# A fused Hawk and RWKV layer on one core: the channel mix's key by seven products, x added by an accumulating DMA, engine order by a table

## The chip, the core and the metric

The kernel runs on one core of a Trainium2 chip. The core has a matrix engine (TensorE, PE in the profile, with PEld for its weight loads), a vector engine (VectorE, DVE), a scalar engine (ScalarE, ACT), a general engine (GpSimd, POOL) and a queue engine (SyncE, SP). Each engine works through its own list of instructions in order; semaphores tie the lists together. PE writes into eight accumulation banks of 128 x 512 fp32 (PSUM); everything else lies in on-chip memory (SBUF). The metric is the device time of one launch in microseconds (us), lower is better: the median of three runs before the change is 652.33 (652.04 to 652.97).

## What is computed

Eight samples of 1024 tokens with 256 channels. Each sample is normalized, and two branches of the normalized input are added to x. The reference, cut to what matters:

```python
def hawk(xn):                                  # 384 hidden channels
    gate = xn @ Wg.T;  u = xn @ Wi.T
    y = causal_depthwise_conv(u, conv_w) + conv_b          # 4 taps
    ig = sigmoid(y @ lru_Wi.T + lru_bi)
    rg = sigmoid(y @ lru_Wg.T + lru_bg)
    alpha = exp(-8 * softplus(lam) * rg)
    beta = sqrt(1 - alpha**2 + 1e-6)
    h = scan(h = alpha * h + beta * ig * y)    # along the tokens
    return (gelu(gate) * h) @ Wo.T

def channel_mix(xn):                           # 256 channels
    xr = mu_r * xn + (1 - mu_r) * previous_token(xn)
    xk = mu_k * xn + (1 - mu_k) * previous_token(xn)
    r = sigmoid(xr @ W_r.T)
    k = relu(xk @ W_k.T) ** 2
    return r * (k @ W_v.T)

xn = layernorm(x)
out = x + hawk(xn) + channel_mix(xn)           # fp32 throughout
```

## The kernel before

**Layout and rounds.** Hidden channels lie on the 128 partitions and tokens along the free axis, in two halves of 512 (`HALVES`). The kernel goes through one round per sample: a first round (sample 0), six middle ones and a last one. Round s computes u, gate, key, r and v products of sample s and the first two of three `l` groups, transposes and normalizes sample s+1, and finishes the recurrence and output products of sample s-1 (`chain`, `outs`). The last round does the whole recurrence of its own sample too.

**Seven products.** The input projections (family "u": Wi and Wg) and the two gate projections (family "l") are taken in pairs of 128 output rows. A pair of rows by two token halves and two channel blocks is a 2x2 block product, computed with seven block products in place of eight (the class `Group`). It needs sums of weight blocks (`weight_sums`) and sums of token blocks (`token_sums`: four subtractions of 128x512 on GpSimd). A group runs in steps on PE: step 1 starts the banks A and C; `seed` (ScalarE) copies A into a new bank B, and `five` copies C into SBUF; step 2 finishes A and adds to B; `fork_c` (VectorE) writes B + five into C; step 3 adds to B and C; `fork_d` writes B + five into the fourth output; step 4 finishes B. `evict` moves a finished bank out on ScalarE and gives it back. "l" has a third channel block, which is added plainly, and so a bank D and a step 5. The key of the channel mix is computed plainly: `key` takes a bank and two products for each of two row blocks and two halves, `key_relu` evicts it, `key_square` squares a half.

**Output.** `r_tanh` writes tanh of r into `tf`, which is the memory of the token sums `xsum`. `value` (VectorE) multiplies it by the v product. `load_again` loads x a second time into `res`, `add_value` adds 0.5 x `tf` to it, and `add_hawk` adds the output product and issues the store.

**Order.** There is no scheduler. `at(t, f)` notes a step at a time t, in units of one 128x512 product; `pe` notes a step of PE at a running clock; at the end all steps are sorted by t and called, and each appends its instructions to the lists of its engines. So the times in `at` only set the order within an engine. In the kernel before, they are offsets written out by hand beside each step: for example the lines `at(4.05, x_sums)`, `mixing(4.2, 5.5, "k")`, and in `Group.step` an eviction 0.1 after the product that ends it. Banks are handed out first in, first out (`take`, `give`), in the order in which steps are called.

**Start.** Before the first round, sample 0 is loaded, its first half normalized and transposed; the second half follows inside the first round (`prepare(1)`, `turn(1)` at 3.99, which copies the transposed half into `xnT`, one channel block on ScalarE and one on VectorE).

Of the kernel before, what the change touches and what calls it, by code (L numbers as in the profile page):

```python
# [12 lines left out]
P = 128  # L13
# [6 lines left out]
HC = 3  # L20
# [9 lines left out]


@with_exitstack
def kernel(
# [47 lines left out]
    ress = [fixed(f"res{n}", [TT, D]) for n in range(2)]  # L81
# [9 lines left out]


    xsum = fixed("xsum", [4, NT])
    ysum = fixed("ysum", [4, NT])
    tf = xsum.rearrange("p a b -> p (a b)").rearrange("p (t d) -> p t d", d=D)
# [54 lines left out]
    ROWS = {"i": ("u", 0), "g": ("u", HC), "lg": ("l", 0), "li": ("l", HC)}  # L150
    families = {"u": fixed("w_u", [DC, 2 * HC * P]), "l": fixed("w_l", [HC, 2 * HC * P])}
    sums = {n: fixed(f"sum_{n}", [4, HC, P]) for n in families}
# [5 lines left out]
    def rows_of(pair, apart):  # L158
        return (pair, pair + HC) if apart else (2 * pair, 2 * pair + 1)

# [11 lines left out]
    def token_sums(dst, b11, b12, b21, b22, pair=None):  # L172

        nc.gpsimd.tensor_tensor(dst[:, 0, :], b12, b11, ALU.subtract)  # L174
        nc.gpsimd.tensor_tensor(dst[:, 2, :], b22, dst[:, 0, :], ALU.subtract)
        nc.gpsimd.tensor_tensor(dst[:, 1, :], b22, b12, ALU.subtract)
        nc.gpsimd.tensor_tensor(dst[:, 3, :], b21, dst[:, 2, :], ALU.subtract)
# [8 lines left out]
    end_of = {}  # L186

    def at(t, f, *args):
        steps.append((t, len(steps), f, args))

    def pe(name, length, f, *args):
        at(clock[0], f, *args)
        clock[0] += length
        end_of[name] = clock[0]
# [4 lines left out]
    class Group:  # L199
# [7 lines left out]

        def step(self, n):
# [9 lines left out]
            def s1():  # L218
                bank["A"], bank["C"] = take(), take()
                product(bank["A"], A(0, 0), chunk(0, 0), start=True)  # L220
                product(bank["C"], S[0], T[:, 0, :], start=True)
# [10 lines left out]
            def s2():  # L232
                product(bank["A"], A(0, 1), chunk(1, 0))
                if third:
                    product(bank["A"], A(0, 2), third(0))
                product(bank["B"], S[1], T[:, 2, :])

            def fork_c():
                nc.vector.tensor_tensor(banks[bank["C"]], banks[bank["B"]], self.five, ALU.add)  # L239

            def s3():
                product(bank["B"], S[2], T[:, 1, :])
                product(bank["C"], S[3], chunk(1, 1))
                if third:
                    product(bank["C"], A(0, 2), third(1))
# [9 lines left out]
            def s4():  # L255
                product(bank["B"], A(1, 1), T[:, 3, :])
                if third:
                    product(bank["B"], A(1, 2), third(0))

            def s5():  # L260
                product(bank["D"], A(1, 2), third(1))
# [6 lines left out]
            if n == 1:  # L268
                pe(f"{self.name}.1", 2, s1)
                at(t + 1.1, seed)  # L270
                at(t + 2.1, five)
            elif n == 2:
                pe(f"{self.name}.2", 2 + extra, s2)
                at(t + 1.1 + extra, evict, "A", 0, 0)
                at(now() + 0.1, fork_c)
                self.after_c = now() + 0.1
            elif n == 3:
                assert t > self.after_c
                pe(f"{self.name}.3", 2 + extra, s3)
                at(t + 1.1, fork_d)  # L280
                self.after_d = t + 1.1
                at(now() + 0.1, evict, "C", 0, 1)
                if not third:
                    at(t + 2.0, self.out, 1, 1, "sbuf")
            elif n == 4:
                assert t > self.after_d
                pe(f"{self.name}.4", 1 + extra, s4)
                at(now() + 0.1, evict, "B", 1, 0)
            else:
                assert t > self.after_d  # L290
                pe(f"{self.name}.5", 1, s5)
                at(now() + 0.1, evict, "D", 1, 1)

    def plain(name, family, pair, chunk, chunks, out):


        def one(r, h):
            b = held[r, h] = take()
            for c in range(chunks):
                product(b, block(family, 2 * pair + r, c), chunk(c, h), start=(c == 0))  # L300

        def evict(r, h):
            b = held.pop((r, h))
            out(r, h, banks[b])
            give(b)

        held = {}
        for h in range(2):
            for r in range(2):
                pe(f"{name}.{r}{h}", chunks, one, r, h)  # L310
                at(now() + 0.1, evict, r, h)
# [27 lines left out]
    def u_group(s, gi):  # L339
        place = u_out(s)  # L340
        return Group(
            f"u{gi}_{s}",
# [4 lines left out]
            xsum,  # L347
# [3 lines left out]
    def l_group(s, gi):  # L351
        rows = rows_of(gi, s == B - 1)
        return Group(
            f"l{gi}_{s}",
# [4 lines left out]
            ysum,  # L359
            lambda r, h, src: l_out(rows[r], h, src),  # L360
            third=lambda h: y[:, 2, HALVES[h]],
        )

# [6 lines left out]

    def load_again(s):
        nc.sync.dma_start(ress[s % 2], x[s].rearrange("(t p) d -> p t d", p=P))
# [52 lines left out]
    def x_sums():  # L425
        def half(c, h):
            return xnT[:, c, 1 + h * NT : 1 + (h + 1) * NT]

        token_sums(xsum, half(0, 0), half(0, 1), half(1, 0), half(1, 1))

    def y_sums():
        def half(c, h):
            return y[:, c, HALVES[h]]

        token_sums(ysum, half(0, 0), half(0, 1), half(1, 0), half(1, 1))
# [16 lines left out]
    def key(m, h):  # L452
        b = take()
        for c in range(DC):
            product(b, weights["k"][:, c, m * P : (m + 1) * P], mixes["k"][:, c, HALVES[h]], start=(c == 0))
        kbank[m, h] = b

    kbank = {}

    def key_relu(s, m, h):  # L460
        ka = key_home(s)
        b = kbank.pop((m, h))
        nc.scalar.activation(ka[:, m, HALVES[h]], banks[b], AF.Relu)
        give(b)

# [4 lines left out]
    def by_token(w, lhs, t, chunks, abreast=False):  # L470

        b = take()
        order = [(j, c) for j in range(2) for c in range(chunks)]
        if abreast:
            order.sort(key=lambda jc: jc[1])
        for j, c in order:
            nc.tensor.matmul(  # L477
                banks[b][:, j * D : (j + 1) * D],
                lhs[:, c, (t + j) * P : (t + j + 1) * P],
                weights[w][:, c, :],  # L480
                start=(j == 0 and c == 0),
                stop=True,
                skip_group_check=True,
            )
        return b
# [6 lines left out]
    def r_product(t):  # L492
        token_bank["r", t] = by_token("r", mixes["r"], t, DC)

    def r_tanh(t):
        b = token_bank.pop(("r", t))
        nc.scalar.activation(tf[:, t : t + 2, :], two_tiles(b), AF.Tanh, scale=0.5)
        give(b)

    def v_product(s, t):  # L500
        token_bank["v", t] = by_token("v", key_home(s), t, DC)

    def value(t):
        b = token_bank.pop(("v", t))
        o = tf[:, t : t + 2, :]
# [3 lines left out]
    def add_value(s, h):  # L509
        o = ress[s % 2][:, 4 * h : 4 * h + 4, :]  # L510
        nc.vector.scalar_tensor_tensor(o, tf[:, 4 * h : 4 * h + 4, :], 0.5, o, ALU.mult, ALU.add)

    def o_product(s, t):
        token_bank["o", s, t] = by_token("o", gs[s % 2], t, HC, s == B - 1 and t == 0)

    def add_hawk(s, t, pieces=1):
        b = token_bank.pop(("o", s, t))
        n = 2 // pieces
        for j in range(0, 2, n):
            o = ress[s % 2][:, t + j : t + j + n, :]  # L520
# [58 lines left out]
    def tp(s):  # L579
        for h in range(2):  # L580
            for c in range(DC):
                pe(f"t{c}{h}_{s}", 0.5, transposes, s, c, h)
                at(now() + 0.1, put_transposed, s, c, h)

    def keys(s, h, m):
        pe(f"k{m}{h}_{s}", 2, key, m, h)
        at(now() + 0.1, key_relu, s, m, h)
        if m == 1:
            at(now() + 0.7, key_square, s, h)

    def gates(s, t):
        pe(f"r{t}_{s}", 2, r_product, t)
        at(now() + 0.1, r_tanh, t)

    def values(s, t, add=0.6):
        pe(f"v{t}_{s}", 2, v_product, s, t)
        at(now() + 0.1, value, t)
        if t % 4 == 2:
            at(now() + add, add_value, s, t // 4)

    def outs(s, t, pieces=1, add=0):
        pe(f"o{t}_{s}", 3, o_product, s, t)
# [32 lines left out]
    with tc.manual_schedule():  # L635
# [50 lines left out]
        busy(4)  # L686
        at(0.02, parameters)
# [3 lines left out]
        at(4.05, x_sums)  # L691
        mixing(4.2, 5.5, "k")
        mixing(12.2, 18.2, "r")
        clock[0] = 0.0
        rate = None
        lgs = {}
        for s in range(B):
            b = now()
            first, last = s == 0, s == B - 1
            us = [u_group(s, n) for n in range(3)]  # L700
            ls = [l_group(s, n) for n in range(3)]
            before = lgs.get(s - 1)
            if first:
# [4 lines left out]
                keys(s, 0, 0)  # L708
                us[2].step(2)
                us[1].step(3)  # L710
                keys(s, 0, 1)
                us[2].step(3)
                us[1].step(4)
                keys(s, 1, 0)
                us[2].step(4)
                keys(s, 1, 1)
                gates(s, 0)
                gates(s, 2)
            else:
# [6 lines left out]
                keys(s, 0, 0)  # L726
                us[0].step(3)
                us[1].step(2)
                keys(s, 0, 1)
# [3 lines left out]
                keys(s, 1, 0)  # L733
                us[2].step(2)
                us[1].step(4)
                keys(s, 1, 1)
                us[2].step(3)
                gates(s, 0)
                gates(s, 2)
                us[2].step(4)  # L740
            at(b + 30, load_again, s)
# [9 lines left out]
            if not last:  # L751
# [6 lines left out]
                at(now() - 0.1, y_sums)  # L758
# [9 lines left out]
                if s + 2 < B:  # L768
# [4 lines left out]
                    at(now() + 11.3, stats, s + 2, 0, 4)  # L773
# [147 lines left out]
```

## Time and profile before

| | |
|---|---|
| time, median of three runs | 652.33 us (652.04 to 652.97) |
| profiled execution, its own time | 652.18 us |
| its span, first to last instruction | 650.4 us |
| granted TensorE clock | 1.000 |
| a middle round (266.31 to 345.52): length | 79.21 us |
| busy in it: PE, DVE, ACT, POOL | 79.21, 57.51, 53.58, 12.58 us |
| bytes read from and written to HBM | 19.94 MB, 8.39 MB |
| loads of x for the sum (`res`), from SP | 8 of 1024 KB, 5.5 us each to landing |

The span is the time between the first and the last instruction of the profiled execution; 1.8 us of the execution lie around it. A row of a timeline reads: start, length, engine, line of the kernel, operation, written tile <- read tiles, shapes, count of merged instructions, and in brackets the idle time before it with what ended it. A row of the chain of waits reads: start, length, engine, tile, line, count. A 128x512 product in fp32 appears as two MATMUL records. Ends of matmuls are modelled, so starts are the safer numbers on PE.

### The profile page before, as it was taken

How to read it: one execution, taken by the hardware profiler on the slowest of the kernel's cores; microseconds unless marked ns; L12 is line 12 of the kernel's file. 1: busy time of each engine (PE TensorE's matmuls, PEld its weight loads, DVE VectorE, ACT ScalarE, POOL GpSimd, SP SyncE). 2: the span in 40 equal slices, each digit the busy share in tenths (PEclk: the TensorE clock that was granted, in tenths of full speed). 3: DMA queues.
4: the chain of work that ended last, by engine and by line, in shares of the span. 5: the costliest groups of instructions: out<-in, count | busy, mean ns of one | idle time of the engine just before them, and what ended most of it. 6: DMA issues, size and time to landing. Idle time of an engine off the chain costs nothing.

```text
span 650.4 us, 5894 instructions
## 1 busy us (share of the span) xinstructions
PE 644.3 (99%) x2048; PEld 375.5 (58%) x2048; DVE 471.2 (72%) x602; ACT 431.9 (66%) x616; POOL 117.5 (18%) x86
## 2 busy tenths in 40 slices
PE   8999999999999999999999999999999999999997
PEld 4466445864468544675447754487544865457466
DVE  4787869846797557966589565994759945699487
ACT  3786878358773687826888178872788537883680
POOL 3705200430004300043000330022300323104000
PEclk9999999999999999999999999999999999999999
DMA  9401200032000310014000140001200012000003
GB/s 316 137 2 37 93 0 1 30 100 65 0 1 33 107 55 1 1 44 142 9 0 1 48 147 0 0 1 48 82 1 1 1 48 82 0 0 1 1 18 113
DMA packets 27550, 28.71 MB, mean 44 GB/s; under 512 B 1152, under 2 KB 27008, under 8 KB 27520
## 3 DMA queue, kind: packets, MB, share of 16 engines
q1 hardware_dynamic: 27104, 27.92, 13.2%
q10 hardware_dynamic: 416, 0.41, 0.2%
q8 instruction: 16, 0.26, 0.2%
q14 instruction: 14, 0.11, 0.1%
HBM read 19.94 MB, written 8.39 MB: 44 GB/s over the span
## 4 chain that ended last, share of the span: by engine, by line
PE 97%; DVE 2%; ACT 0%; issue 0%; DVEq 0%
PE bank L180 64%; PE bank L477 30%; PE bank L403 2%; PE bank L660 1%; DVE y L540 0%; DVE xr L448 0%; DVE st L376 0%; DVE g L253 0%; ACT x L398 0%; DVE half_b L678 0%; DVE bank L239 0%; DVE xnT L420 0%; ACT xnT L422 0%; ACT u L323 0%; DVE mv L378 0%
## 5 line engine op out<-in xcount | busy, mean ns | idle before, releaser
L180 PE MATMUL bank<-y,w_l 128*128 128x512 f32 x288 | 137.8, 592 | 0.0
L540 DVE SCALAR_TENSOR_TENSOR y<-u,par,y 128x1024 f32<-128x1024 f32 x72 | 94.3, 1326 | 1.2
L180 PEld LDWEIGHTS bank<-y,w_l 128*128 128x128 f32 x288 | 54.6, 190 | 62.7 <-issue 60.8
L477 PE MATMUL bank<-w_o,g 128*128 128x256 f32 x384 | 86.1, 379 | 0.0
L174 POOL TENSOR_TENSOR ysum<-y 128x512 f32<-128x512 f32 x8 | 16.9, 2114 | 368.3 <-PE bank L477 341.3
L477 PEld LDWEIGHTS bank<-w_o,g 128*128 128x128 f32 x384 | 73.0, 190 | 15.9 <-issue 5.3
L180 PE MATMUL bank<-ysum,sum_l 128*128 128x512 f32 x144 | 72.1, 592 | 0.0
L225 ACT COPY bank<-bank 128x512 f32<-128x512 f32 x47 | 27.0, 575 | 66.1 <-PE bank L180 65.1
L180 PE MATMUL bank<-xsum,sum_u 128*128 128x512 f32 x138 | 69.1, 592 | 0.0
L239 DVE TENSOR_TENSOR bank<-bank,five 128x512 f32<-128x512 f32 x47 | 32.8, 698 | 49.1 <-PE bank L180 35.4
L335 ACT ACTIVATE tr<-bank,half_b 128x512 f32<-128x512 f32 x48 | 32.8, 684 | 52.3 <-PE bank L180 52.1
L180 PE MATMUL bank<-xk,w_k 128*128 128x512 f32 x128 | 60.1, 592 | 0.0
L477 PE MATMUL bank<-w_r,xr 128*128 128x256 f32 x256 | 57.7, 379 | 0.0
L477 PEld LDWEIGHTS bank<-w_r,xr 128*128 128x128 f32 x256 | 48.6, 190 | 13.1 <-issue 7.0
L180 PE MATMUL bank<-xnT,w_u 128*128 128x512 f32 x108 | 54.1, 593 | 0.2 <-ACT xnT L422 0.2
L477 PE MATMUL bank<-w_v,ysum 128*128 128x256 f32 x224 | 49.5, 379 | 0.0
L477 PEld LDWEIGHTS bank<-w_v,ysum 128*128 128x128 f32 x224 | 42.6, 190 | 5.8
L521 DVE TENSOR_TENSOR res<-res,bank 128x512 f32<-128x512 f32 (+1 forms) x36 | 21.8, 623 | 33.3 <-PE bank L477 33.2
L180 PEld LDWEIGHTS bank<-xsum,sum_u 128*128 128x128 f32 x138 | 26.1, 189 | 33.1 <-issue 31.2
L180 PEld LDWEIGHTS bank<-ysum,sum_l 128*128 128x128 f32 x144 | 26.8, 190 | 30.7 <-issue 28.7
L335 ACT ACTIVATE ti<-bank,half_b 128x512 f32<-128x512 f32 x48 | 30.4, 680 | 18.1 <-PE bank L180 18.1
L180 PEld LDWEIGHTS bank<-xk,w_k 128*128 128x128 f32 x128 | 24.3, 190 | 30.7 <-issue 30.4
(99 smaller groups left out, 1015.0 us busy)
## 6 DMA issues: line engine op xcount, KB each, us to landing
res<-in_x_dram SPq DMA_DIRECT2D x8, 1024.0 KB, 5.5
x<-in_x_dram SPq DMA_DIRECT2D x7, 1024.0 KB, 5.5
out_dram<-res SPq DMA_DIRECT2D x28, 256.0 KB, 2.1
x<-in_x_dram SPq DMA_DIRECT2D x4, 256.0 KB, 4.4
out_dram<-res SPq DMA_DIRECT2D x8, 128.0 KB, 2.0
w_l<-in_lru_wg_dram SPq DMA_DIRECT2D x1, 576.0 KB, 6.1
w_l<-in_lru_wi_dram SPq DMA_DIRECT2D x1, 576.0 KB, 7.1
w_u<-in_w_i_dram ACTq DMA_DIRECT2D x1, 384.0 KB, 3.9
```

What stands on the lines that cost most here:

```text
L174: nc.gpsimd.tensor_tensor(dst[:, 0, :], b12, b11, ALU.subtract)
L180: nc.tensor.matmul(banks[b], lhsT, rhs, start=start, stop=True, skip_group_check=True)
L225: nc.scalar.copy(banks[bank["B"]], banks[bank["A"]])
L239: nc.vector.tensor_tensor(banks[bank["C"]], banks[bank["B"]], self.five, ALU.add)
L335: nc.scalar.activation(dst[:, m, HALVES[h]], src, AF.Tanh, bias=half_b[:, b + m : b + m + 1], scale=0.5)
L403: nc.tensor.matmul(banks[b][:, t * P : (t + 1) * P], xs[s % 2][:, 4 * h + t, c * P : (c + 1) * P], ident, is_transpose=True, start=(t == 0 ...
L477: nc.tensor.matmul(banks[b][:, j * D : (j + 1) * D], lhs[:, c, (t + j) * P : (t + j + 1) * P], weights[w][:, c, :], start=(j == 0 and c == 0),
L521: nc.vector.tensor_tensor(o, o, two_tiles(b)[:, j : j + n, :], ALU.add)
L540: nc.vector.scalar_tensor_tensor(y[:, m, :], u[:, m, k : k + S], column(COL_CONV_W + k * HC + m), y[:, m, :], ALU.mult, ALU.add,)
L660: nc.tensor.matmul(banks[b], warm[:, 0:P], warm, start=True, stop=True)
```

## The change

Three things change together.

*The key.* A family "k" is added: `k_group` is a `Group` of one pair of rows, with `weight_sums("k")` once and four token sums of xk in each round (`k_sum`), one of them in place in `xk`. The fourth output gets its relu from SBUF (`late`). `token_sums` becomes `token_sum`, one subtraction per step, so that each of the four has its own place. Steps of PE are noted product by product.

*The sum with x.* `r_tanh` writes into one of two buffers `sides`, which no longer share memory with `xsum`. W_v is halved once (`halve`, on GpSimd), `value` leaves the channel mix's output in `sides`, and `add_x` adds x to it with a DMA from GpSimd's queue that accumulates in its destination. `load_again` and `add_value` are gone; `add_hawk` adds to `sides` and stores from there.

*The order.* `at` looks a step up by name in a table, `PLACES`, one part for the first round, one for the middle ones and one for the last; where it finds the name, the place in the table, counted from the round's start, is used in place of the hand-written time. Steps noted before the first round are called "early" and have no place there. The order of PE is as before but for the key's steps and one exchange (u2's step 3 with the first r product).

```diff
+PLACES = {
+    "first": {
+        "u0_0 evict 0 0": 2.36, "u0_0 evict 1 0": 3.48, "u0_0 evict 0 1": 6.36, "u1 seed": 9.36,
...
+        "u2 evict A 0 0": 21.18, "inverse 0 8": 21.66, "u1 evict C 0 1": 21.86, "k fork_c": 22.36,
+        "k evict A 0 0": 22.54, "conv_first 2": 23.22, "u2 fork_d": 23.36, "conv_rest 0 1": 24.17,
...
+        "k fork_d": 26.36, "normalize 1 1": 26.64, "conv_rest 0 2": 27.17, "k late": 27.34,
...
+    "middle": {
+        "gated_input 0": -0.83, "beta 0": 0.33, "stats 0 1": 0.59, "stats 1 1": 1.32, "u0 seed": 1.56,
...
+        "l2 evict B 1 0": 7.56, "u0 fork_c": 7.63, "gated_state 0": 8.44, "l2 evict D 1 1": 9.16,
...
+        "x_sum 0": 66.54, "mix_before k 0": 67.06, "x_sum 2": 67.7, "mix_before k 1": 68.29,
+        "mix k 0": 68.87, "l0 evict C 0 1": 69.51, "mix_before r 0": 70.31, "mix k 1": 70.36,
+        "mix_before r 1": 71.52, "x_sum 1": 71.84, "add_hawk 6 1": 71.84, "decay 0": 72.75,
+        "mix r 0": 73.01, "l0 evict B 1 0": 74.09, "mix r 1": 74.5, "decay_square 0": 74.89,
+        "k_sum 0": 76.0, "l1 evict A 0 0": 76.0, "l1 fork_c": 76.36, "decay_rest 0": 77.17,
+        "l0 evict D 1 1": 77.36, "k_sum 1": 77.97, "decay 1": 78.23, "x_sum 3": 79.13, "l2 seed": 79.57,
...
+        "own scaled_input 2 L": 90.88, "own recur 2 L": 91.74, "own gated_state 2 L": 93.26,
...
-    ress = [fixed(f"res{n}", [TT, D]) for n in range(2)]
+    sides = [fixed(f"side{n}", [TT, D]) for n in range(2)]
...
-    tf = xsum.rearrange("p a b -> p (a b)").rearrange("p (t d) -> p t d", d=D)
+
+    ksum = [fixed(f"ksum{n}", [NT]) for n in range(3)]
+    ksum.insert(1, mixes["k"][:, 0, HALVES[1]])
...
+    def halve(name):
+        nc.gpsimd.tensor_scalar(weights[name], weights[name], 0.5, None, ALU.mult)
...
-    def token_sums(dst, b11, b12, b21, b22, pair=None):
-
-        nc.gpsimd.tensor_tensor(dst[:, 0, :], b12, b11, ALU.subtract)
-        nc.gpsimd.tensor_tensor(dst[:, 2, :], b22, dst[:, 0, :], ALU.subtract)
-        nc.gpsimd.tensor_tensor(dst[:, 1, :], b22, b12, ALU.subtract)
-        nc.gpsimd.tensor_tensor(dst[:, 3, :], b21, dst[:, 2, :], ALU.subtract)
+    def token_sum(i, dst, half):
+
+        o, a, b = (
+            (0, half(0, 1), half(0, 0)),
+            (2, half(1, 1), dst[0]),
+            (1, half(1, 1), half(0, 1)),
+            (3, half(1, 0), dst[2]),
+        )[i]
+        nc.gpsimd.tensor_tensor(dst[o], a, b, ALU.subtract)
...
-    def at(t, f, *args):
-        steps.append((t, len(steps), f, args))
...
+    def at(t, f, *args, of=""):
+        shown = args[1:] if f.__code__.co_varnames[:1] == ("s",) else args
+        shown = ["LR"[a.start // NT] if isinstance(a, slice) else str(a) for a in shown]
+        name = " ".join([of or era[0], f.__name__, *shown]).strip()
+        if name in places:
+            t = base[0] + places[name]
+        steps.append((t, len(steps), f, args, name))
...
+    def k_group(s):
+        ka = key_home(s)
+
+        def place(r, h, src):
+            dst = ka[:, r, HALVES[h]]
+            if src is None:
+                return dst
+            nc.scalar.activation(dst, dst if isinstance(src, str) else src, AF.Relu)
+            squared[s, h] = squared.get((s, h), 0) + 1
+            if squared[s, h] == 2:
+                key_square(s, h)
+
+        return Group("k", "k", 0, (0, 1), lambda c, h: mixes["k"][:, c, HALVES[h]], ksum, place)
...
+    def k_sum(i):
+        token_sum(i, ksum, lambda c, h: mixes["k"][:, c, HALVES[h]])
...
-    def load_again(s):
-        nc.sync.dma_start(ress[s % 2], x[s].rearrange("(t p) d -> p t d", p=P))
...
-    def add_value(s, h):
-        o = ress[s % 2][:, 4 * h : 4 * h + 4, :]
-        nc.vector.scalar_tensor_tensor(o, tf[:, 4 * h : 4 * h + 4, :], 0.5, o, ALU.mult, ALU.add)
...
+    def add_x(s):
+        rows = x[s].rearrange("(t p) d -> p t d", p=P)
+        nc.gpsimd.dma_start(sides[s % 2], rows, accum_op=ALU.add)
...
+        for i in range(4):
+            at(9 + i / 10, k_sum, i)
         mixing(12.2, 18.2, "r")
+        at(8, halve, "v")
+        at(1.5, weight_sums, "k")
...
                 us[1].step(1)
-                keys(s, 0, 0)
+                ks.step(1)
                 us[0].step(3)
                 us[1].step(2)
-                keys(s, 0, 1)
+                ks.step(2)
                 us[0].step(4)
                 us[2].step(1)
                 us[1].step(3)
-                keys(s, 1, 0)
+                ks.step(3)
                 us[2].step(2)
                 us[1].step(4)
-                keys(s, 1, 1)
+                ks.step(4)
+                gates(s, 0)
                 us[2].step(3)
-                gates(s, 0)
                 gates(s, 2)
                 us[2].step(4)
-            at(b + 30, load_again, s)
```

## The prediction

> **What bounds the kernel now.** I read four views: the page, the waits of PE, the chain of waits in order of time, and the timelines of three places. Times are microseconds (us).
>
> ```profile
> PE 644.3 (99%) x2048; PEld 375.5 (58%) x2048; DVE 471.2 (72%) x602; ACT 431.9 (66%) x616; POOL 117.5 (18%) x86
> ...
> PE 97%; DVE 2%; ACT 0%; issue 0%; DVEq 0%
> ...
> L180 PE MATMUL bank<-xk,w_k 128*128 128x512 f32 x128 | 60.1, 592 | 0.0
> ```
>
> PE is busy for 99% of the span, and the chain that ended last is PE for 97%. A modelled busy time alone would not prove it, so the waits of PE come next: who was waited for, in total, times, longest.
>
> ```profile
> PE bank L660 <- DVE five L636: 1.2, 1, 1.2
> PE bank L180 <- DVE g L253: 0.9, 1, 0.9
> PE bank L403 <- DVE x L396: 0.3, 1, 0.3
> PE bank L180 <- ACT xnT L422: 0.2, 1, 0.2
> ```
>
> That is all: 2.6 us, all of it in the first 37 us. From 36.97 to 646.9 PE never stops. The price of a product is read from the chain of waits (start, length, what):
>
> ```profile
> 301.75 43.77 PE bank L180 x102
> ```
>
> A 128x512 product is two records, so 51 products in 43.77 us: 0.858 us each. I call that a **unit**. (The row's mean of 592 ns per record overlaps its neighbour and must not be multiplied.) 16 records of the key per sample, x128 in all, are 8 products. A middle round has 92 units and takes 79.21 us (266.31 to 345.52).
>
> **The removed product.** Seven products in place of eight, for 8 samples: 8 x 0.858 = **-6.87 us**, and all of it lies on the path, since nothing else ends later. Where PE stops being last nothing more is gained, so the rest of the sum asks where ACT, DVE or POOL become late.
>
> **The first round, a stall that goes.** PE's timeline:
>
> ```profile
> 16.11 4.56 PE L180 MATMUL bank<-xnT,w_u 128*128 128x512 f32 x10 [0.24 <-ACT xnT L422]
> ...
> 34.24 1.88 PE L180 MATMUL bank<-xk,w_k 128*128 128x512 f32 x4
> 36.97 1.13 PE L180 MATMUL bank<-xsum,w_u 128*128 128x512 f32 x2 [0.85 <-DVE g L253]
> ```
>
> Two products from 34.24 are done at 35.96, the next begins at 36.97: 1.01 us lost. u2's step 4 waits for its `fork_d`, which on DVE stands behind `mix r` and two `conv_rest`. The table puts `u2 fork_d` (23.36) ahead of the convolution (from 24.17). Walked with the rows' durations it ends near 33.8, due at 36.4. **-1.01 us.** What is late next there: `k fork_d`, done near 36.4 and due at 37.2.
>
> **The first round, a start that slips.** ACT's timeline:
>
> ```profile
> 14.96 0.56 ACT L323 COPY u<-bank 128x512 f32<-128x512 f32 x1
> 15.47 0.59 ACT L422 COPY xnT<-bank 128x512 f32<-128x512 f32 x1
> 15.95 0.59 ACT L323 COPY u<-bank 128x512 f32<-128x512 f32 x1
> ```
>
> PE's product at 16.11 waited for the xnT copy in the middle. The table puts the eviction `u0_0 evict 1 0` at 3.48, ahead of `turn` at 3.99, so two u copies stand before it: one step of 15.47 to 15.95, **+0.5 us**. Nothing covers it.
>
> **POOL in the first round.** Added ahead of k's step 1: four sums of w_k, `halve` of w_v and four k sums. The sums of w_u end at 12.3 and xnT comes at 16.5 now, so four sums of a third of their 1.0 us fit between. The x sums ended at 22.8, now 23.3; `halve` (no row; a 128x512 sum alone takes 1.09, two inputs, so at most that if no lock is met) to 24.4; k sum 0 to 25.5. PE's product that reads it is due 11 units after 16.6, at 26.0: margin 0.5. The other end, both delayed by the 1.1 us of a DVE turn (below), would be 27.7: +1.7 us. I take 0, as DVE then does bn_stats, beside which the sums of w_u stayed at 1.00. Should `halve` have to wait for w_v: issued at 6.97 and landing 9.4 later, it is there at 16.4.
>
> **The added k sums and the lock, in each middle round.** This is the place that decides. Four k sums join four x sums on POOL just as DVE mixes xk and xr. DVE, POOL and PE in that stretch of one round:
>
> ```profile
> 298.41 2.04 DVE L448 SCALAR_TENSOR_TENSOR xk<-xnT,par,xk 128x1024 f32<-128x1024 f32 x1 [0.17 <-ACT xk L442]
> 302.39 1.33 DVE L448 SCALAR_TENSOR_TENSOR xk<-xnT,par,xk 128x1024 f32<-128x1024 f32 x1
> 303.64 2.47 DVE L448 SCALAR_TENSOR_TENSOR xr<-xnT,par,xr 128x1024 f32<-128x1024 f32 x2
> 306.08 0.70 DVE L239 TENSOR_TENSOR bank<-bank,five 128x512 f32<-128x512 f32 x1
> ```
> ```profile
> 298.28 1.09 POOL L175 TENSOR_TENSOR xsum<-xnT,xsum 128x512 f32<-128x512 f32 x1
> 299.33 2.25 POOL L176 TENSOR_TENSOR xsum<-xnT 128x512 f32<-128x512 f32 x1
> ```
> ```profile
> 307.59 1.88 PE L180 MATMUL bank<-ysum,sum_l 128*128 128x512 f32 x4
> ```
>
> The mix begun at 298.41 ends 1.08 after POOL's sum ended (299.37), and POOL's next, begun at 299.33, ends 1.13 after the mix. They take turns. By the row's mean (four mixes in 5.84 us, as now) the four k sums cost DVE nothing and `l1 fork_c`, the line at 306.08, stays there. The Trainium skill ("SBUF — State Buffer", Who interferes with whom) speaks against that: a DVE instruction with two SBUF inputs and a GpSimd instruction that reads SBUF exclude each other for the whole instruction. With POOL never idle, each mix then waits a POOL turn, 2.2 us apiece. Walked so: x sum 0 ends 298.45, x sum 2 299.55, mix k0 300.65, x sum 1 301.75, mix k1 302.85, `add_hawk` 6 (one input in PSUM, no lock) 303.5, k sum 0 303.95, mix r0 305.05, k sum 1 306.15, mix r1 307.25, `l1 fork_c` 307.95. It is due at l1's step 3, the second product of the line at 307.59: 308.45. I take the rule, since single rows show it. The margin shrinks from 1.67 to 0.5 us and no stall follows: **0**. A further turn would cost 1.1 - 0.5 = 0.6 us in each of 6 middle rounds.
>
> **Other edits, with what hides them.** DVE in a middle round: 57.5 us now, less two `add_value` (2.33 + 2.22), plus two forks at 0.70: 54.4 and turns of the lock, in a round of 91 units, 78.35 us. ACT: 53.6, plus a seed and a five (0.57 + 0.59), plus two more table loads (the order of instructions has 5 in a middle round for 3) at 1.28: 57.3. Relus and squares are as many as before. The tightest place on ACT is the start of a round: three betas at 1.14, seed, five, one eviction, a table load, then l2's three evictions moved behind them. Counted from the round's start, l2's first is done at 7.0, and k's step 1 takes that bank at 10 units, 8.6: margin 1.6. On DVE `k fork_d` ends at 21.4, due at 27 units, 23.2. PE's waits for banks and forks are new there, and behind each waits the whole rest of the round; by these margins none of them counts.
>
> **x by an accumulating DMA.** SP loses eight loads of 1 MB; what stands behind them in its queue only comes sooner. POOL gains eight DMAs, of a kind that the trace lacks. Nearest row: the same megabyte from SP lands in 5.5 us and takes 0.6 to issue. "DMA: Bandwidth & Descriptors" (Bandwidth) gives 6.15 us for the transfer alone when GpSimd issues it, and no price for the adding. Say 5.5 to 12. Its reader is `add_hawk` on DVE, behind which mixes and forks queue that PE waits for; but it comes some 90 units later, in the last round 38 units (33 us). If it holds POOL, x sum 0 stands behind it: issued near 45 us of the round, xnT ready at 57.3, and the eight sums are done 7 us before the next round needs them, so up to 19 us of holding is hidden. Both ends: 0.
>
> **The end.** In the last round `gated_state 2 L` is done 0.9 us before the product that reads it, and after the last product the same two pieces are added and written (3.5 us now). 0.
>
> **Sum** against the profiled execution's own 652.18 (span 650.4): -6.87 - 1.01 + 0.5 = -7.4, so 644.8. That execution lies 0.15 under the median of 652.33, hence **645.0**.
>
> **Rivals.** (1) *One more turn of the lock*, or another margin of about half a us that is missed each round: 6 x 0.6 to 0.7 = 4 us, so 649. For it: a margin of 0.5 after ten chained steps. Against: a mix whose POOL partner comes late saves a full turn as easily. (2) *Slower: DVE two turns behind.* At `l1 fork_c`, two more POOL turns cost 6 x (2.2 - 0.5) = 10.2 us: 655. It decides from a delay of 0.5 + 7.4/6 = 1.7 us per round on. Against: POOL has only two sums that can run before DVE reaches the fork. (3) *POOL held over 19 us by the DMA*: each us beyond costs 7 us; at 20 us 652, no change. The rows for a megabyte stand against it. (4) *The seven products don't save a product*: added seeds wait for PE itself; then only the first round's 0.5 is gained, 651.8. PE's order of instructions has 7, against it.
>
> **How the numbers follow.** Forecast, 644 to 646.5 (the high end is the delayed k sum 0): 0.67. Rival 1, 646.5 to 650.5: 0.23. Rival 2: 0.04; rivals 3 and 4: 0.03 each. The low end is 644.0: the start slips less, and half a us of spread. The high end 648.8 takes in most of rival 1. Within 0.2% is 1.3 us, about what these runs can tell from nothing. Rival 4 and half of rival 3 are no change: 0.04; slower, rival 2 and the rest of 3: 0.05; faster 0.91.
>
> **What would show it.** Middle rounds of 78.35 us in the chain; no line of PE's waits that recurs six times; 112 records of the key in all; first PE product after the second transposes near 16.6; `l1 fork_c` ending about 1.2 us later than now against PE. A wait of PE on DVE at l1's step 3, six times, is rival 1 or 2; on POOL, rival 3. I am wrong if PE shows recurring waits anywhere else, above all at the round's start.

## The result, and the profile after

The changed kernel takes **645.19 us** (median of four runs, 645.16 to 645.58) where the kernel before took 652.23 in the same session (652.04 to 652.97): a ratio of 0.9891, 95% interval 0.9874 to 0.9908. The forecast was 645.0. The profiled execution is one of 645.16 us with a span of 643.2, at a granted clock of 1.0.

The page first: busy time, the chain that ended last by engine, two DMA rows (queue, count, KB each, us from issue to landing).

```profile
PE 637.7 (99%) x2032; PEld 372.6 (58%) x2032; DVE 469.5 (73%) x602; ACT 458.9 (71%) x646; POOL 186.4 (29%) x131
...
PE 98%; DVE 1%; ACT 0%; issue 0%; DVEq 0%
...
side<-in_x_dram POOLq DMA_DIRECT2D x8, 1024.0 KB, 11.0
...
out_dram<-side SPq DMA_DIRECT2D x28, 256.0 KB, 3.6
```

PE has 16 records fewer, which are the eight products. Its busy time fell by 6.6 us, and it is still the chain: everything else that grew (ScalarE by 27 us, GpSimd by 69) stayed beside it. The last two rows are the price of the accumulating DMA: 11.0 us to landing, where the plain load from SP took 5.5, and the stores beside it 3.6 for 2.1 (2.1 again in experiment 3, which goes without that DMA). Whether anything waits for them is asked of PE's waits (who was waited for: us in total, times, longest):

```profile
PE bank L776 <- DVE five L752: 1.2, 1, 1.2
PE bank L305 <- ACT xnT L560: 0.7, 1, 0.7
```

One wait on `fork_d` (0.85 us in the first round) has gone, and so has one of 0.3 on VectorE's normalize at the start; one on the xnT copy has grown from 0.2 to 0.7, and nothing recurs. So there is no new bound in the middle rounds. One of them, 260.75 to 339.10 (length; busy PE, PEld, DVE, ACT, POOL; clock, DMA share, GB/s):

```profile
260.75:339.10 78.35, 78.35 (x251) 46.10 (x251) 57.74 (x72) 57.41 (x82) 20.81 (x13) 1.00 0.17 41
```

Its length was 79.21 us before. Where the 7.2 us of span went can be read off the starts of the 16 transposes of each round in the chain of waits, which split the span the same way in both kernels:

| stretch | before | after | difference |
|---|---|---|---|
| to the first product behind the second turn | 16.11 | 16.61 | +0.50 |
| from there to the first round's transposes | 43.60 | 41.67 | -1.93 |
| six rounds between transposes | 472.69 | 467.69 | -5.00 |
| from the last of these to the end | 118.0 | 117.2 | -0.8 |
| span | 650.4 | 643.2 | -7.2 |

### The profile page after: what moved, and what is told of

Read it like the earlier page. It is cut to its first block, busy times and chain, and to the rows that moved or that the text cites. A ratio compares the mean times of both kernels' runs of the same rounds, so it can differ in the third digit from the quotient of the medians.

```text
span 643.2 us, 5932 instructions
## 1 busy us (share of the span) xinstructions
PE 637.7 (99%) x2032; PEld 372.6 (58%) x2032; DVE 469.5 (73%) x602; ACT 458.9 (71%) x646; POOL 186.4 (29%) x131
## 4 chain that ended last, share of the span: by engine, by line
PE 98%; DVE 1%; ACT 0%; issue 0%; DVEq 0%
PE bank L305 65%; PE bank L594 30%; PE bank L541 2%; PE bank L776 1%; DVE st L514 0%; ACT x L536 0%; ACT u L445 0%; DVE xnT L558 0%; ACT xnT L560 0%; DVE mv L516 0%; DVE side L639 0%; DVE mv L527 0%; DVEq L1048 0%; ACT std L519 0%; DVE five L752 0%
## 5 line engine op out<-in xcount | busy, mean ns | idle before, releaser
L302 POOL TENSOR_TENSOR ysum<-y 128x512 f32<-128x512 f32 x16 | 24.2, 1513 | 298.1 <-PE bank L594 277.6
L658 DVE SCALAR_TENSOR_TENSOR y<-u,par,y 128x1024 f32<-128x1024 f32 x72 | 88.8, 1288 | 0.0
L536 ACT ACTIVATE x<-x,mv,std 128x256 f32<-128x256 f32 x60 | 31.6, 591 | 52.0 <-DVE mv L527 52.0
L368 DVE TENSOR_TENSOR bank<-bank,five 128x512 f32<-128x512 f32 x55 | 38.0, 691 | 38.5 <-PE bank L305 38.5
L639 DVE TENSOR_TENSOR side<-side,bank 128x512 f32<-128x512 f32 (+1 forms) x36 | 22.1, 624 | 41.8 <-PE bank L594 41.8
L376 DVE TENSOR_TENSOR bank<-bank,five 128x512 f32<-128x512 f32 x24 | 16.8, 699 | 44.8 <-PE bank L305 44.8
L360 ACT COPY bank<-bank 128x512 f32<-128x512 f32 x55 | 31.7, 577 | 22.9 <-PE bank L305 22.2
L302 POOL TENSOR_TENSOR xsum<-xnT 128x512 f32<-128x512 f32 x16 | 21.1, 1331 | 84.4 <-ACT xnT L560 84.4
```

The lines of the kernel that those rows point to most:

```text
L302: nc.gpsimd.tensor_tensor(dst[o], a, b, ALU.subtract)
L360: nc.scalar.copy(banks[bank["B"]], banks[bank["A"]])
L376: nc.vector.tensor_tensor(d, banks[bank["B"]], self.five, ALU.add)
L536: nc.scalar.activation(xa, xa, AF.Identity, bias=m, scale=r)
L639: nc.vector.tensor_tensor(o, o, two_tiles(b)[:, j : j + n, :], ALU.add)
L658: nc.vector.scalar_tensor_tensor(y[:, m, :], u[:, m, k : k + S], column(COL_CONV_W + k * HC + m), y[:, m, :], ALU.mult, ALU.add,)
```

## Experiments

Where tenths matter I give the spans of all executions of a kernel beside the median of its times, because the spans scatter less: the kernel after had 13 executions in three sessions, with spans of 643.1 to 644.0, mean 643.4.

**1. The eighth product put back, all else kept.** The table's places behind it move by one unit.

```diff
-                ks.step(1)
+                keys(s, 0, 0)
...
-                ks.step(4)
+                keys(s, 1, 1)
...
-            at(9 + i / 10, k_sum, i)
```

> The changed kernel with the key computed plainly again (eight products, no k sums), everything else kept: the table with later places shifted by one unit, and the accumulating DMA. My theory (PE never stops, so a product taken out is worth its 0.858 us in each of 8 rounds): +6.9 us, 652.1 us, and middle rounds of 79.2 us. Rival (the gain came from the table and the first round, the product is worth little): below 648 us.

Measured: 651.64 us (650.4 to 652.48 in 20 runs), 0.9991 [0.9984, 0.9998] of before; span 649.8 against 643.2. Its rounds are 79.21 us again (135.67 to 214.88), with no recurring wait. So the key's product carries nearly the whole gain. The table and the DMA alone are worth about half a us, with an interval of 0.1 to 1.0. The profiled executions say where it lies: the start is 0.47 us later than before, the stretch from there to the first round's transposes 1.12 shorter, and the rest the same within 0.1.

**2. How near the lock brings the fork to its due time.** In the kernel after, VectorE and GpSimd take turns in the stretch where the k sums join the mixes; the prediction calls this the lock. Here I only moved `l1 fork_c` behind the one VectorE instruction that follows it.

```diff
-"l1 fork_c": 76.36, "decay_rest 0": 77.17,
+"l1 fork_c": 77.18, "decay_rest 0": 77.17,
```

> The changed kernel with one place moved in the middle rounds: l1's fork_c (77.18 for 76.36) stands behind the first decay_rest, that is one more VectorE instruction in the stretch where the k sums run. My theory (the two engines exclude each other for whole instructions, so decay_rest first waits for the GpSimd sum that got its turn at 303.5 and ends near 305.15 on the changed kernel's clock; fork_c then ends near 305.8 where 304.60 is due): a wait of PE of about 1.2 us in each of 6 middle rounds, 652.4 us. Rival (no turns, decay_rest costs its own 0.69 us, so fork_c ends near 304.95): 0.35 us in each, 647.3 us. Rival (fork_c has far more slack than the margin of 0.35 us that is read): 645.2 us.

Measured: 653.02 us (651.72 to 653.67 in 12 runs), 1.0011 [1.0002, 1.0019] of before: one instruction of 1.5 us in each middle round takes the whole gain back (the kernel after took 645.83 in the same session). First PE's wait, then the end of the chain before it (start, length, what), then PE's row:

```profile
PE bank L305 <- DVE bank L368: 6.2, 6, 1.0
```
```profile
296.83 4.16 DVE xk L580 x2
300.99 0.60 DVE side L639
301.59 3.84 DVE xr L580 x2
305.43 1.50 DVE q L675
306.93 0.62 DVE bank L368
```
```profile
307.59 1.13 PE L305 MATMUL bank<-ysum,sum_l 128*128 128x512 f32 x2 [1.05 <-DVE bank L368]
308.55 1.02 PE L305 MATMUL bank<-y,sum_l 128*128 128x512 f32 x2
```

Two mixes take 4.16 and two take 3.84 us, not the 1.46 apiece of before (four in 5.84). By the sum of these rows, short mixes would have ended the fork at 305.4, in time for 306.38, in spite of the instruction put ahead of it. That the k sums make them long can be read off experiment 1, which has the same order without k sums. Its two mixes of xr at this place:

```profile
302.89 2.71 DVE L599 SCALAR_TENSOR_TENSOR xr<-xnT,par,xr 128x1024 f32<-128x1024 f32 x2
```

The instruction that was moved ahead of the fork took 0.68 us there and 1.50 here.

A round is 79.65 us long, 1.3 more, though PE's wait is 1.05. The product would have started at 306.38 (305.52, where the one before it started, and 0.858); it came 1.21 later, and the next one 0.96 after it rather than 0.86. These 1.21 and 0.10 are the 1.3. The number in brackets is smaller because it counts from the modelled end of the row before, and a row of two records is 1.02 us long where the next one can start after 0.858. So a stop is measured from start to start; experiment 6 has it again.

**3. x without the accumulating DMA.** SP loads x into `side`, VectorE adds it in two instructions, and tanh of r goes back into the memory of `xsum`.

```diff
-        nc.gpsimd.dma_start(sides[s % 2], rows, accum_op=ALU.add)
+        for h in range(2):
+            o = sides[s % 2][:, 4 * h : 4 * h + 4, :]
+            nc.vector.tensor_tensor(o, tf[:, 4 * h : 4 * h + 4, :], o, ALU.add)
+    def load_again(s):
+        nc.sync.dma_start(sides[s % 2], x[s].rearrange("(t p) d -> p t d", p=P))
```

> The changed kernel with x loaded again from SP by a plain DMA into the side buffer and added on VectorE (two 128x1024 additions per round, at the place of the accumulating DMA), r's tanh and the values back in the memory of the token sums; seven products and the table kept. My theory (the accumulating DMA and the removed additions both lie beside PE): 645.2 us, within 0.5. Rival (part of the gain is the DMA's, since it frees VectorE): 647 us or more, with new waits of PE.

Measured: 644.94 us (644.86 to 645.07). PE's waits are the same two, the megabyte lands in 5.4 us, and a middle round is 78.3 us with VectorE busy for 59.87 of it instead of 57.74. VectorE has that room, so the accumulating DMA brings no time here, and its 11 us cost none that could be told: spans of 642.8 to 643.1 beside a mean of 643.4.

**4. The convolution ahead of the fork, in the first round.** This undoes the one place that the prediction held responsible for the stall that goes.

```diff
-"u2 fork_d": 23.36, "conv_rest 0 1": 24.17,
+"u2 fork_d": 23.36, "conv_rest 0 1": 23.34,
...
-"conv_rest 0 2": 27.17,
+"conv_rest 0 2": 23.35,
```

> The changed kernel with the first round's places of two convolution steps moved (23.34 and 23.35 for 24.17 and 27.17), so that they stand ahead of u2's fork_d on VectorE as in the kernel before. My theory (that order made the stall of 1.0 us in the first round before): PE waits for u2's fork_d again, 0.7 to 1.5 us, once: 646 to 646.7 us. Rival (that stall had another cause, and the table removed it otherwise): 645.2 us.

Measured: 646.5 us (646.01 to 647.14), beside 645.83 (645.41 to 645.98) for the kernel after in the same session. The profiled execution is the longest of the four, with a span of 645.1. PE's rows at the place:

```profile
35.29 1.88 PE L305 MATMUL bank<-xk,sum_k 128*128 128x512 f32 x4
38.06 1.13 PE L305 MATMUL bank<-xsum,w_u 128*128 128x512 f32 x2 [0.90 <-DVE g L376]
39.28 1.10 PE L305 MATMUL bank<-ksum,w_k 128*128 128x512 f32 x2
```

The two products from 35.29 end at 37.01, the next starts at 38.06: 1.05 us. The stop of before is back, with its size. A second one follows, which the kernel before could not have: `k fork_d`, now also behind the convolution, ends at 39.14, and its product starts at 39.28 and not at 38.92. With 0.49 us from a later start (17.10 for 16.61) these are the 1.9 us by which this span exceeds 643.2.

**5. The start's xnT copy ahead of the u copies.** Two places of the table are moved behind `turn`, run in two sessions.

```diff
-"u0_0 evict 0 0": 2.36, "u0_0 evict 1 0": 3.48,
+"u0_0 evict 0 0": 4.01, "u0_0 evict 1 0": 4.02,
```

> The changed kernel with two places moved: both u0_0 evictions of the first half stand behind the turn (4.01 and 4.02 for 2.36 and 3.48). My theory (the start of the first round's second half hangs on the xnT copy on ScalarE, which waits behind two u copies): the first product after the transposes starts near 16.0 instead of 16.6 us, so 644.6 us. Rival (the other xnT copy on VectorE or the k sums set the pace, so that PE loses later what it gains): 645.2 us, no change.

> The version with both u0_0 evictions behind the turn once more, now beside the changed kernel. Its span was 0.5 us shorter, its time was not. If the saved half a us is real time: 644.7 beside 645.2 us. If it is given back outside the first and last instruction: both 645.2 us, with a gap between time and span of about 2.5 us here and 2.0 us there.

Measured: 645.30 (645.07 to 645.33) and 644.31 us (644.25 to 645.78). The wait is back to its size of before:

```profile
16.22 4.13 PE L305 MATMUL bank<-xnT,w_u 128*128 128x512 f32 x9 [0.24 <-ACT xnT L560]
```

The two runs differ by a us, and the place of the difference can be seen. The 26 warm-up products at the very start took 8.40 us in the first and 7.47 in the second, and everything behind them shifted, so that this product started at 16.22 and at 15.18. The times cannot settle half a us against that; the distance from ScalarE's normalize of the second half to this product can. It is 2.16 and 2.15 us here, 2.15 before, and 2.59 in the kernel after and in every experiment that kept its start. The order of the copies costs **0.44 us**.

The kernel after was repeated for comparison in two sessions:

> The changed kernel itself, unchanged, on the same chip and in the same rounds as the next three, so that half a us can be told: 645.2 us, as it was.

> The kernel after, unchanged, beside the early statistics on the same chip: 645.2 to 645.8 as before, the distance from ScalarE's normalize of the second half to the first product behind it 2.59 us.

It took 645.83 (645.41 to 645.98; ratio 0.9898 [0.9884, 0.9913]) and 646.01 us (645.06 to 646.45; 0.9909 [0.9895, 0.9923]), the distance 2.59 in the latter.

**6. The order written by hand, with seven products.** The table is left empty.

```diff
-        places.update(PLACES["first"])
-            places.update(PLACES["first" if first else "last" if last else "middle"])
```

> The changed kernel with an empty table, so that the hand-written times set the order; seven products and accumulating DMA kept. My theory (the key's forks need their places: with three scaled inputs and four scans ahead of them on VectorE, the walk gives k's fork_d about 0.8 to 1 us late in each middle and the last round, and the first round's fork stall of about 1 us or more is back, less 0.5 for the start): 649 to 655 us, with recurring waits of PE for the forks. Rival (the table is worth only the first round's half a us): 645 to 646.5 us.

Measured: 660.0 us (659.06 to 660.28), 1.0118 [1.0098, 1.0139] of before. The direction was expected, the size was not. The span of the profiled execution is 657.7 us, 14.5 more than after. The middle rounds are 79.34 us, 1.0 longer each; the six stretches between transposes and the end together make 6.1 of it. The other 8.4 us come from the first round, whose transposes start at 66.69 instead of 58.28. VectorE puts three convolutions ahead of a fork, which starts at 31.55. VectorE's row, and PE's rows at its two waits:

```profile
24.92 6.70 DVE L658 SCALAR_TENSOR_TENSOR y<-u,par,y 128x1024 f32<-128x1024 f32 x3
```
```profile
32.29 1.13 PE L305 MATMUL bank<-xsum,sum_u 128*128 128x512 f32 x2 [1.19 <-DVE bank L368]
40.12 3.75 PE L305 MATMUL bank<-xk,sum_k 128*128 128x512 f32 x4 [4.78 <-DVE bank L368]
43.66 1.91 PE L305 MATMUL bank<-xsum,w_u 128*128 128x512 f32 x2
45.37 1.43 PE L305 MATMUL bank<-ksum,w_k 128*128 128x512 f32 x2
```

The first product behind the second turn came at 15.35 here, 1.3 us earlier than after, so 9.7 us are to be found. From start to start the two stops are 1.35 and 5.05 us, 6.4 of them, and the two products after the first stop came 0.2 late. The rest stands in the rows from 40.12 on: four records take 3.75 us, where four of the same kind take 1.88 elsewhere. From 40.12 to the next row of another line, at 46.64, four products take 6.52 us where four units are 3.43: 3.1 us. The same place in windows (columns as for the middle round above; the clock is third from the end):

```profile
40.00:42.00 2.00, 1.88 (x3) 0.88 (x4) 2.00 (x3) 1.40 (x3) 0.00 (x0) 0.50 0.00 0
...
44.00:46.00 2.00, 2.00 (x3) 0.68 (x3) 1.97 (x3) 1.97 (x4) 0.00 (x0) 0.50 0.00 0
46.00:50.00 4.00, 4.00 (x18) 3.17 (x17) 3.23 (x17) 3.35 (x5) 0.00 (x0) 0.98 0.00 0
```

After some 5 us without work PE was given half its clock for some 6 us of work, which costs these 3.1 us, and the 9.7 are complete. It is what the Trainium skill ("TensorE: Matmul & The Clock Gate", Why this matters for your kernels) warns of, idle gaps above some 3 us between bursts. Where the limit lies no run here shows; the stop of 1.35 us left the clock at 1.00. The walk behind the expectation had only the wait.

**7. A start with earlier statistics.** The kernel's remaining loss is ahead of 17 us. The statistics of sample 0's second half go ahead of the first transposes, the second turn comes two products earlier, and four of the 26 warm-up products are left out.

```diff
-        busy(26)
+        busy(22)
         prepare(0)
+        prepare(1)
         turn(0)
...
-        at(0.05, prepare, 1)
-        at(3.99, turn, 1)
+        at(0.05, scale, 1)
+        at(1.99, turn, 1)
```

(`prepare(1)` no longer contains the normalize; that is `scale`.)

> The kernel after with only its start changed: 22 instead of 26 warm-up products, sample 0's statistics of the second half made ahead of the transposes of the first half (VectorE idles 2.52 us there before its xnT copy at 10.48), and the turn of the second half two products earlier. Theory: from its first product after the second turn on PE has no gap, so whatever the start saves is saved at the end: that product at about 14.4 us instead of 16.61, time about 643.0. Rival A: the later rounds are bound by something beside PE's amount of work, as the sums of GpSimd or the mixes: a recurring wait of PE appears or the time stays at 645.2. Rival B: the four warm-up products left out are paid back by a lower clock in the first round (granted clock under 1.00 between 8 and 20 us): 645 to 646.

Measured: 644.71 us (644.26 to 644.82) where the kernel after took 646.01 on the same chip; spans of 641.9 to 642.4. The expected 643.0 was wrong by a plain slip: the product at 14.24 is no longer the first one behind the turn, because the earlier turn moved two products of the first half behind it. Comparable is 14.24 + 2 x 0.858 = 15.96. It also showed a new wait of 0.55 us: ScalarE's root of the second half stood ahead of its xnT copy of the first. The clock was 1.00 from 8 us on, and from 9.26 us on the products came at their usual pace (four warm-ups in 1.03 us, as after), so no lower clock paid for the warm-ups left out.

**8. The same, mended, with 22 and with 26 warm-up products.** The root goes behind the xnT copy, and the two u evictions behind `turn` as in experiment 5.

```diff
-        prepare(0)
-        prepare(1)
+        measure(0)
+        scale(0)
+        measure(1)
         turn(0)
...
-        at(0.05, scale, 1)
+        at(0.01, scale, 1)
...
-        busy(22)
+        busy(26)
```

(`measure` is the statistics, `scale` is root, inverse and normalize; the last hunk is the second kernel's.)

> Early statistics again, with what the run before showed mended: ScalarE's root of the second half stands behind its xnT copy of the first (it had held that copy back, and PE 0.55 us with it), and the two early u evictions stand behind turn. What counts is the first product that reads the second half. In the kernel after that is the one at 16.61 (17.02 in the third run of it). In the early statistics two products of the first half were moved behind the second turn, a thing that my 14.4 left out, so its comparable start is 14.24 + 2 x 0.858 = 15.96, and its span fell by what that says. Theory, start chain: PE runs from 10.3 to that product with at most 0.4 us of gap, the product comes at about 15.1, the span falls to 641.5 to 642.1, time about 643.7. Rival: other steps of the start (evictions on ScalarE, banks) give it back, then a new wait of PE before 40 us and 644.7 or more.

> The same mended start with all 26 warm-up products, to tell the order from the four products left out. If the order alone brings it, the time is that of the mended start with 22 (within 0.3 us). If the warm-ups stand on the path themselves, the first product of the second half comes later[...] to about 16.0, and so does the end: 644.6. If the four left out were paid for by a lower clock, this one is the faster.

Measured: **644.15** (643.9 to 644.25) with 22 and **644.17** us (643.77 to 644.38) with 26; ratios to before 0.9877 [0.9860, 0.9893] and 0.9878 [0.9863, 0.9892]. All eight spans are 641.6 to 641.9, below all thirteen of the kernel after (643.1 to 644.0): 1.6 us on the means. VectorE and PE with 22 warm-ups:

```profile
11.46 1.51 DVE L534 TENSOR_SCALAR x<-x,std,mv 128x256 f32<-128x256 f32 x2
```
```profile
12.56 1.34 PE L541 MATMUL bank<-ident,x 128*128 128x128 f32 x8 [0.59 <-DVE x L534]
13.74 6.17 PE L305 MATMUL bank<-xnT,w_u 128*128 128x512 f32 x14
```

With 26 the last row starts at 13.59, not later but 0.15 earlier. The second half's chain is comparable at 13.74 + 1.72 = 15.46 us and at 15.31 where it was 16.61. So order brings the gain: that of the statistics, of the second turn, and of the u copies, which experiment 5 puts at 0.44 us. The four warm-up products are off the path: with 22, PE only waits for VectorE instead. Of the two outcomes named for 26 it was the first, not 644.6. With 22 the product came 0.4 us later than expected, and PE's gap was 0.59 where at most 0.4 was allowed. By its median this is the fastest kernel of the study. Its lead over experiment 5's second run (644.31, spans from 641.7) is not clear of the scatter of the start, and the kernel after was not run beside these two, where the spans of before were 650.2 to 650.4. A normalize pair takes 1.51 us where the first half's took 0.74. GpSimd's sums of the weights run at the same time and are the likely cause; no run tests it.

## Why the prediction held, point by point

**The removed product** (-6.87 by the prediction). The rounds give 0.86 each where they can be compared (79.21 to 78.35). Six of them together give 5.00 rather than 5.15, because the one from 58.28 to 134.22 shortened by 0.68 only. Its 0.18 is a cost that the prediction did not have. The end of the first round has the same meeting of k sums, mixes and `l1 fork_c` as the middle rounds, and its margin was not worked out. VectorE's fork and PE's rows there:

```profile
68.71 0.69 DVE L368 TENSOR_TENSOR bank<-bank,five 128x512 f32<-128x512 f32 x1
```
```profile
68.51 2.06 PE L305 MATMUL bank<-ysum,sum_l 128*128 128x512 f32 x4
70.41 1.02 PE L305 MATMUL bank<-y,sum_l 128*128 128x512 f32 x2
```

The fork ends at 69.40 and is due at 68.51 + 0.858 = 69.37. From 68.51 to 70.41 are 1.90 us where two units are 1.72: the missing 0.18. The stop is too short for the list of waits. The two repeats of the kernel after have it too (rows of 2.07 and 2.06); experiment 1, which has no k sums, does not (1.88).

**The stall that goes** (-1.01) and its cause, `fork_d` behind the convolution, are shown by experiment 4. First round: -1.93 where 0.86 and 1.01 make 1.87. PE's rows in the first round of the kernel after:

```profile
34.79 1.88 PE L305 MATMUL bank<-xk,sum_k 128*128 128x512 f32 x4
36.51 1.02 PE L305 MATMUL bank<-xsum,w_u 128*128 128x512 f32 x2
```

34.79 + 2 x 0.858 = 36.51: no gap. `u2 fork_d` ended at 34.05 (the walk said 33.8), `k fork_d` at 37.08 with its product at 37.37 (36.4 and 37.2). Late next was what the prediction named, with 0.3 us to spare.

**The start that slips** (+0.5). The place and the cause hold. Its size is 0.44 by the distance from the normalize; the 0.50 of the two profiles also has the warm-ups in it, and agrees by luck.

**GpSimd in the first round** (0; other end +1.7). The right outcome, with luck, and with a term sized too small. The prediction put `halve` below the 1.09 of a sum with two inputs. It has one input and took more:

```profile
23.31 1.49 POOL L281 TENSOR_SCALAR w_v<-w_v 128x512 f32<-128x512 f32 x1
24.79 1.26 POOL L302 TENSOR_TENSOR ksum<-xk 128x512 f32<-128x512 f32 x1
```

So k sum 0 was ready at 26.05 and not at 25.5, and its product started at 26.16, one unit behind the one before it: the margin of 0.5 was 0.1. "A nearest row with more inputs" is not an upper bound.

**The lock in each middle round** (0; margin 0.5). This is the term on which the rule and the mean differed most, and the rule described the rows. VectorE and GpSimd after:

```profile
295.05 4.15 DVE L580 SCALAR_TENSOR_TENSOR xk<-xnT,par,xk 128x1024 f32<-128x1024 f32 x2 [0.66 <-ACT xk L574]
...
299.72 3.92 DVE L580 SCALAR_TENSOR_TENSOR xr<-xnT,par,xr 128x1024 f32<-128x1024 f32 x2
303.56 0.69 DVE L368 TENSOR_TENSOR bank<-bank,five 128x512 f32<-128x512 f32 x1
```
```profile
298.08 2.25 POOL L302 TENSOR_TENSOR ksum<-xk 128x512 f32<-128x512 f32 x1
300.41 2.15 POOL L302 TENSOR_TENSOR ksum<-xk,ksum 128x512 f32<-128x512 f32 x1
```

Four mixes took 8.07 us in place of the 5.84 of before (predicted: turns of 2.2 apiece), and GpSimd's sums show the same 2.15 and 2.25, each with a turn of VectorE in it. Without k sums, in experiment 1, the four took 4.15 and 2.71; so the k sums cost 1.2 us of the 2.2, and the rest came with the new order. `l1 fork_c` ends at 304.25 and is due at 304.60, the second product of PE's line at 303.74. The margin is 0.35 where 1.67 had been and 0.5 was predicted. Experiment 2 shows that it is real: a delay of 1.5 us, more than 0.35 and less than 1.67, costs all that the seven products bring.

**ScalarE, VectorE and the round's start** (0). ScalarE is busy for 57.41 us a round (57.3 predicted), VectorE for 57.74 (54.4 and turns), l2's first eviction is done 7.1 us after the round's start (7.0 as worked out). None of these waits shows.

**The accumulating DMA** (0; 5.5 to 12 us to landing, up to 19 us of holding hidden). It lands in 11.0 us and holds GpSimd for 1.55 us, once a round. Experiment 3 shows that taking it away changes no time that could be told.

**The sum** (-7.4) came out as -7.2 in the spans of the two profiled executions; the difference is the 0.18 at the end of the first round. That 645.19 lies so close to 645.0 is luck in part: repeated, the kernel took 645.83 and 646.01, gains of 6.4 and 5.9 in their sessions. The rivals are refuted for this order: in the middle rounds the lock costs no further turn and VectorE isn't two turns behind, GpSimd isn't held for 19 us, and the records of PE are 16 fewer. That a half-us margin is missed each round was a fair rival: it is missed once, by a few hundredths, and experiment 2 is the case where it is missed each time.

Open: what lies around the span is 1.8 us before and in experiment 1, and 2.0 to 2.6 in nearly all executions of the others. The accumulating DMA is not the cause: experiment 1 has it at 1.8, experiment 3 lacks it at 2.0. No experiment was aimed at that. It is why medians of the kernel after reach 646.0 while its spans stay near 643.4.

## What to carry to other kernels

Where one engine is gapless, work taken off it is gained in full as long as every other engine's due times still hold; so the working goes into margins, in us, at the places where two engines take turns. For an instruction that shares a lock use single rows with and without a partner, never the group's mean. And when the middle has no waits left, look at the prelude: there, some 1.6 us of span came from order alone (experiment 8), with no work removed.

## What the hardware showed that was not expected

- PE after some 5 us without work ran at half clock for some 6 us (experiment 6: clock 0.50 from 40 to 46, four records in 3.75 us for 1.88).
- The same 26 warm-up products took 7.11 to 8.40 us in the profiled executions of these kernels, and shifted what stands behind them, except in experiment 8, where VectorE's chain is later than they are. The first of them come 0.43 us apart and the last 0.22; what differs is when the pace changes. From 4 to 5 us the kernel after (8.40) has four records of them, experiment 2 (7.11) six. The clock column reads 1.00 in both, so it does not show this.
- GpSimd's multiplication by a constant, one input of 128x512, took 1.49 us in each kernel that had no mix on VectorE beside it (in experiment 6 VectorE was idle then), and 2.46 in experiments 7 and 8, where a mix ran; a subtraction of two inputs without a partner took 1.09 to 1.28.
- A stop of PE is longer than the wait in brackets: experiment 2's waits of 1.05 made rounds 1.3 us longer. Experiment 6's two waits a round, 0.4 together, are 0.72 from start to start and made rounds 1.0 longer, because the next product comes some 0.1 late as well.
